# A conditioned two-layer block kernel in fp32: all LayerNorms and ssm products first, then the MLP by pairs of blocks

## The chip, the core and the metric

The kernel runs on one core of one Trainium2 chip. The metric is the device time of one execution in microseconds (us). The kernel before takes 586.52 us, the median of three runs (586.5 to 586.7). The engines are called as in the profile: PE is TensorE (PEld its weight loads), DVE VectorE, ACT ScalarE, POOL GpSimd and SP SyncE, which here only issues DMAs.

## What is computed

The input x has 2 batches of 2048 tokens of 512 values, and the condition has 512 values for each batch. All is fp32.

```python
emb = silu(cond) @ ada_w + ada_b
shift_msa, scale_msa, gate_msa, shift_mlp, scale_mlp, gate_mlp = split(emb, 6)
norm = ln(x) * (1 + scale_msa) + shift_msa
h = gelu(norm @ ssm_w1 + ssm_b1)               # 512 -> 512, exact gelu
x = x + gate_msa * (h @ ssm_w2 + ssm_b2)       # 512 -> 512
norm2 = ln(x) * (1 + scale_mlp) + shift_mlp
hf = gelu_tanh(norm2 @ ff_w1 + ff_b1)          # 512 -> 1024
x = x + gate_mlp * (hf @ ff_w2 + ff_b2)        # 1024 -> 512
```

Each of the two LayerNorms works over the 512 values of a token. Four matrix products follow: ssm1, ssm2, ff1 and ff2 below.

## The kernel before, in words

**Blocks.** The 4096 tokens are worked on in eight blocks of 512 (i = 0 to 7), four for each batch. A block's x is one SBUF tile of 128 x 4 x 512. The gates are folded into the weights w2 and fw2, which is done again for the second batch.

**A LayerNorm** (class Norm) has six steps: `stats` (DVE, bn_stats L511, one for each quarter c of the block; for block 1 they are shared with ACT, L525 to L534), `scales` (eight small operations on POOL, L580 to L598, that give rstd and -mean*rstd), `normal` (ACT, L612, four), `turn` (DVE, a transpose of 32 x 32 blocks, L623, four), `move` (L632, sixteen DMAs of 64 KB that carry the turned blocks to their partitions, issued by SP or by SP and ACT), `modulate` (ACT, L661, four, with shift and scale). What comes out has the features on the partitions.

**Products.** ssm1 and ssm2 use one Strassen level in Winograd's form: seven products P1 to P7 of four matmuls each, 128 x 256, in three PSUM banks (y, x, v) that are read and summed on as the products come (`group`, L474). The sums of operands that this needs are single tensor_tensor operations on DVE or POOL (L347). ff1 of block 0 is done in the same way, in two groups. From block 1 on, ff1 is `Second.products` (L1024): 26 products of two matmuls each, whose operands come from two lists of sums, HK_A for the weight (made once) and HK_B for the tokens (each block, L962). ff2 is `residual_in_leaves` from block 1 on: one Strassen level, of which P1 and P6 stay plain (L817, 16 matmuls of 256 columns) and the five others are split once more (L863, 70 matmuls of 128 columns).

**Order.** The order on every engine is written out by hand: each product group has hooks, lists of operations that are issued behind a named product. The blocks are interleaved: behind ff1 of block i comes ssm2 of block i+1, then ff2 of block i, then ssm1 of block i+2. So a block's normalisation, its sums and its DMAs lie beside other blocks' products. [...]

**Start.** Some idle matmuls (L1117) come first. Then the conditioning products (L274, "pada", sixteen small matmuls for each of six parts of ada_w), which need ada_w from DRAM. A gate product (L309, "pgate") copies the gate of batch 0 to all partitions.

**Lines that the prediction names:** L274 pada, L309 pgate, L395 folding of a gate into a weight, L474 ssm products, L817 plain and L863 split parts of ff2, L877 and L913 the readings of ff2's PSUM into x, L927 the last outputs, L1024 ff1.

Of the kernel before, what the change touches and what calls it, by code (L numbers as in the profile page):

```python
# [8 lines left out]
F32 = mybir.dt.float32  # L37
# [4 lines left out]

HK_A = [
    (1, '-', 1, 0),
    (3, '+', 3, 1),
    (11, 'n', 10, 11),
    (27, '+', 11, 1),
    (26, '-', 27, 8),  # L50
    (25, '+', 13, 15),
    (25, '-', 25, 12),
    (24, '-', 27, 2),
    (23, '-', 3, 24),
    (8, '+', 8, 23),
    (8, '+', 0, 8),
    (22, '-', 12, 26),
    (21, 'n', 1, 22),
    (22, '+', 2, 22),
    (9, '-', 9, 11),  # L60
    (20, '-', 6, 27),
    (10, '+', 6, 10),
    (19, '-', 9, 10),
    (19, 'n', 26, 19),
    (0, '-', 4, 0),
    (23, '-', 23, 0),
    (4, '+', 4, 27),
    (27, '-', 6, 19),
    (2, '-', 27, 2),
    (5, '+', 5, 11),  # L70
    (5, '-', 5, 4),
    (27, '+', 19, 25),
    (27, '-', 27, 5),
    (18, '+', 15, 1),
    (14, '+', 14, 15),
    (15, '-', 21, 14),
    (6, '-', 6, 11),
    (14, '-', 14, 27),
    (7, 'n', 7, 6),
    (6, '+', 7, 27),  # L80
    (6, 'n', 23, 6),
    (13, '-', 13, 5),
]
HK_B = [
    (23, '-', 4, 6),
    (22, '-', 0, 23),
    (21, '+', 1, 3),
    (20, '-', 21, 22),
    (19, '-', 7, 21),
    (18, '-', 5, 21),  # L90
    (17, '+', 3, 23),
    (16, '-', 18, 23),
    (15, '-', 19, 16),
    (14, '-', 17, 15),
    (13, '-', 20, 14),
    (0, '+', 0, 16),
    (12, '-', 6, 21),
    (11, '+', 2, 23),
    (1, '+', 1, 12),
    (10, '-', 11, 20),  # L100
    (9, '-', 12, 10),
    (8, '-', 16, 9),
    (2, '-', 2, 3),
    (7, '-', 6, 7),
]


HK_P = [
    (5, True, 26, 20, ((5, -1), (7, 1))),
    (3, True, 25, 3, ((5, 1), (7, 1))),  # L110
    (0, True, 12, 22, ((6, 1),)),
    (2, True, 1, 13, ((1, -1), (7, -1))),
    (5, False, 8, 21, ((1, 1),)),
    (0, False, 21, 0, ((7, 1),)),
    (1, True, 3, 19, ((1, 1),)),
    (2, False, 20, 15, ((3, -1),)),
    (0, False, 22, 18, ((1, 1),)),
    (3, False, 19, 17, ((5, -1),)),
    (2, False, 10, 14, ((5, 1),)),
    (5, False, 23, 12, ((3, 1),)),  # L120
    (0, False, 24, 16, ((0, 1),)),
    (1, True, 11, 8, ((0, -1), (2, -1))),
    (5, False, 4, 10, ((2, 1),)),
    (0, False, 2, 23, ((4, -1), (5, -1))),
    (3, False, 27, 1, ((3, 1),)),
    (5, False, 0, 9, ((0, 1),)),
    (1, False, 9, 11, ((4, 1),)),
    (4, True, 18, 14, ()),
    (3, False, 5, 2, ((2, 1),)),
    (0, False, 6, 6, ((2, 1),)),  # L130
    (4, False, 15, 5, ((7, -1),)),
    (3, False, 14, 4, ()),
    (0, False, 7, 7, ((3, 1),)),
    (3, False, 13, 11, ((6, 1),)),
]

HK_BANK = {5: "y", 2: "x", 4: "v", 0: "x", 1: "y", 3: "v"}
# [3 lines left out]
def kernel(  # L141
# [20 lines left out]
    KD = D // P  # L162
    KH = H // P
# [5 lines left out]
    NADA = ada_w.shape[1] // D  # L169

    const = ctx.enter_context(tc.tile_pool(name="const", bufs=1))
    big = ctx.enter_context(tc.tile_pool(name="big", bufs=7))
    sums = ctx.enter_context(tc.tile_pool(name="sums", bufs=3))
    work = ctx.enter_context(tc.tile_pool(name="work", bufs=1))
    small = ctx.enter_context(tc.tile_pool(name="small", bufs=3))
    dram = ctx.enter_context(tc.tile_pool(name="dram", bufs=1, space=bass.MemoryType.DRAM))
    ps_t = ctx.enter_context(tc.tile_pool(name="ps_t", bufs=2, space=bass.MemoryType.PSUM))
    ps_g = ctx.enter_context(tc.tile_pool(name="ps_g", bufs=2, space=bass.MemoryType.PSUM))

    ctx.enter_context(tc.manual_schedule())  # L180

# [4 lines left out]
    G = 32  # L186
    IDLE = 5


    R_COND, R_ADA = 0, B * KD  # L190
    R_B1 = R_ADA + NADA * KD
    R_FB1 = R_B1 + KD
    ROWS = R_FB1 + KH
    def big_tile(name):
        return big.tile([P, KD, D], F32, tag="big", name=name)

    xs = {}

    def load_x(i, pieces=1):
        xs[i] = big_tile(f"x_{i}")  # L200
        for s in range(pieces):
            c = slice(s * C // pieces, (s + 1) * C // pieces)
            nc.sync.dma_start(out=xs[i][:, c, :], in_=x_blk[i][:, c, :])

    ada = {}

    def load_ada(g):
        ada[g] = big_tile(f"ada_{g}")
        nc.sync.dma_start(
            out=ada[g], in_=ada_w[:, g * D : (g + 1) * D].rearrange("(k p) n -> p k n", p=P)  # L210
        )

    def load_w(name, w, t=None, eng=nc.sync):
        if t is None:
            t = const.tile([P, w.shape[0] // P, w.shape[1]], F32, tag=name, name=name)
        eng.dma_start(out=t, in_=w.rearrange("(k p) n -> p k n", p=P))
        return t

    def load_half(name, w, t, h):
        K = t.shape[1] // 2  # L220
        nc.sync.dma_start(
            out=t[:, h * K : (h + 1) * K],
            in_=w.rearrange("(h k p) n -> h p k n", h=2, p=P)[h],
        )

    def load_row(t, row):
        nc.sync.dma_start(out=t, in_=row.unsqueeze(0).to_broadcast([P, D]))
        return t


    fw2_t = const.tile([P, 5, 3, KD // 2, P], F32, tag="fw2_t", name="fw2_t")
    brows = fw2_t.rearrange("p a s k d -> p (a s k d)")[:, : KD * D].rearrange("p (k d) -> p k d", k=KD)
    rows = brows[:ROWS, 2, :P]
    nc.scalar.dma_start(out=rows[R_COND:R_ADA, :], in_=cond.rearrange("b (k p) -> (b k) p", p=P))
    nc.scalar.dma_start(out=rows[R_ADA:R_B1, :], in_=ada_b.rearrange("(k p) -> k p", p=P))
    nc.scalar.dma_start(out=rows[R_B1:R_FB1, :], in_=b1.rearrange("(k p) -> k p", p=P))
    nc.scalar.dma_start(out=rows[R_FB1:ROWS, :], in_=fb1.rearrange("(k p) -> k p", p=P))

    ident = const.tile([P, P], F32, tag="ident", name="ident")
    make_identity(nc, ident)  # L240
# [3 lines left out]
    w1_sb = load_w("w1", w1)  # L244
    load_x(1)
    load_ada(2)

    nc.gpsimd.memset(brows[:, :2, :P], 0.0)
    gate_b = {2: brows[:, 0, :P], 5: brows[:, 1, :P]}

    def load_gate_b(g):
        for m in range(P // G):
            row = ada_b[g * D : (g + 1) * D].rearrange("(n m q) -> m n q", n=KD, q=G)[m]
            nc.sync.dma_start(
                out=gate_b[g][m * G : m * G + B, :].rearrange("p (n q) -> p n q", n=KD),
                in_=row.unsqueeze(0).to_broadcast([B, KD, G]),
            )

    w2_sb = load_w("w2", w2)
    load_gate_b(2)  # L260
    b2_bc = work.tile([P, D], F32, tag="gb", name="gb2_0", bufs=2)
    load_row(b2_bc, b2)
    fw1_sb = load_w("fw1", fw1)
    load_ada(3)

    mods = {}

    def rows_of(g):

        pa = ps_g.tile([P, D], F32, tag="x", name=f"pada_{g}")  # L270
        w = ada[g].rearrange("p k (n m q) -> p k m n q", n=KD, q=G)
        for k in range(KD):
            for m in range(P // G):
                nc.tensor.matmul(  # L274
                    pa[m * G : (m + 1) * G, :P],
                    silu[:, k, :],
                    w[:, k, m],
                    start=(k == 0),
                    stop=(k == KD - 1),
                    tile_position=(0, m * G),  # L280
                    skip_group_check=True,
                )
        return pa

    def modulation(g0, part):

        g = g0 + part
        pa = rows_of(g)
        turned = pa[:, P : 2 * P]
        nc.vector.transpose(turned, pa[:, :P])  # L290
        turned = turned.rearrange("p (n q) -> p n q", n=KD)
        m = const.tile([P, KD, B], F32, tag=f"mod_{g0}_{part}", name=f"mod_{g0}_{part}")
        bias = colsT[:, R_ADA + g * KD : R_ADA + (g + 1) * KD]
        nc.vector.tensor_tensor(m, turned[:, :, :B], bias.unsqueeze(2).to_broadcast([P, KD, B]), ALU.add)
        mods[g0, part] = m

    gate, gate_rows = {}, {}

    def gate_rows_of(g, tag):
        pa = rows_of(g)  # L300
        r = work.tile([P, P] if g == 2 else [P, D], F32, tag=tag, name=f"grows_{g}", bufs=1)
        nc.vector.tensor_tensor(r[:, :P], pa[:, :P], gate_b[g], ALU.add)
        gate_rows[g] = r

    def first_ssm_gate():

        pg = ps_t.tile([P, D], F32, tag="t", name="pgate_2_0")
        for m in range(P // G):
            nc.tensor.matmul(  # L309
                pg.rearrange("p (n m q) -> p m n q", n=KD, q=G)[:, m],  # L310
# [62 lines left out]
    def thirds(t):  # L373
        return [t[:, j] for j in range(3)]
# [1165 lines left out]
```

## Time and profile before

| what | value |
|---|---|
| median of 3 runs | 586.52 us (586.5 to 586.7) |
| profiled execution, span from first to last instruction | 583.8 us |
| DMA traffic | 57.54 MB, mean 99 GB/s |
| DVE / ACT / POOL busy | 411.9 / 269.0 / 424.6 us |
| PE instructions recorded | 3287 |
| granted TensorE clock | 1.000 |

The profile is one execution. Its span leaves out what lies ahead of the first and behind the last instruction. A row of the timeline has start, length, engine, line, operation, output<-inputs, shapes and count, and in brackets the idle time ahead of it and who ended it. A row of the chain of work that ended last has start, length and what ran. A row of the groups has busy time and the mean of one in ns behind the count.

### The profile page before, as it was taken

The numbers are of one execution on the slowest core, as the hardware profiler recorded it, in microseconds if no ns is written. First come the engines' busy times: TensorE is split into PE (matmuls) and PEld (weight loads), VectorE is DVE, ScalarE is ACT, GpSimd is POOL, SyncE is SP. The second block draws the span as 40 slices with busy tenths as digits, with TensorE's granted clock in tenths as the row PEclk, the third lists the DMA queues.
The fourth block names the chain that finished last, engine by engine and source line by source line (L and its number), as shares of the span: only waits on it lengthen the run. The fifth ranks groups of instructions, "written<-read, shape, count | busy, mean of one in ns | idle before, by whom it ended". The sixth has DMA issues, their size and how long they took to land.

```text
span 583.8 us, 9508 instructions
## 1 busy us (share of the span) xinstructions
PE 577.3 (99%) x3287; PEld 514.4 (88%) x3287; DVE 411.9 (71%) x748; ACT 269.0 (46%) x495; POOL 424.6 (73%) x516
## 2 busy tenths in 40 slices
PE   9999999999999999999999999999999999999997
PEld 5788888888899888998889988898888998899896
DVE  4867898897867375685756857884756367787676
ACT  2644457405642554435742588235673331731520
POOL 1785249999997938969788799998579445369351
PEclk9999999999999999999999999999999999999999
DMA  8967332303205303472033821243130330031002
GB/s 322 394 186 290 92 72 74 108 37 108 61 15 180 127 0 69 118 213 73 1 90 74 288 73 24 50 122 122 45 72 2 100 118 1 1 72 74 1 1 72
DMA packets 26011, 57.54 MB, mean 99 GB/s; under 512 B 4928, under 2 KB 5996, under 8 KB 24300
## 3 DMA queue, kind: packets, MB, share of 16 engines
q1 hardware_dynamic: 22240, 52.20, 28.4%
q10 hardware_dynamic: 3724, 4.75, 3.3%
q8 instruction: 26, 0.43, 0.3%
q14 instruction: 21, 0.17, 0.1%
HBM read 32.80 MB, written 8.40 MB: 71 GB/s over the span
## 4 chain that ended last, share of the span: by engine, by line
PE 94%; DMA 3%; DVE 2%; issue 0%; ACTq 0%; DVEq 0%
PE px_hC L1024 10%; PE py_oA L474 9%; PE py_hA L474 9%; PE py_hC L1024 8%; PE py_oC L817 8%; PE pv_hC L1024 8%; PE pl_oC_P_y L863 8%; PE pv_oA L474 5%; PE pl_oC_P_v L863 5%; PE pv_hA L474 4%; PE pl_oC_P_x L863 3%; DMA ada<-in_L_cond_ada_w_dram 3%; PE px_oA L474 2%; PE py_oC L474 2%; PE py_hC L474 2%; PE px_hA L474 2%
## 5 line engine op out<-in xcount | busy, mean ns | idle before, releaser
L661 ACT ACTIVATE nT<-nT,mod,mod 128x512 f32<-128x512 f32 x36 | 26.4, 803 | 63.4 <-DMA nT<-blocks 57.2
L347 POOL TENSOR_TENSOR hSC<-hClo,hChi 128x512 f32<-128x512 f32 (+1 forms) x16 | 19.7, 1234 | 41.0 <-ACT hChi L1019 35.6
L962 POOL TENSOR_TENSOR forms<-forms 128x256 f32<-128x256 f32 x56 | 41.8, 746 | 3.3
L511 DVE BATCH_NORM_STATS2 st<-x 128x6 f32<-128x512 f32 x56 | 37.9, 677 | 5.1 <-DMA x<-in_x_dram 4.9
L1024 PE MATMUL py_hC<-forms,fw 128*128 128x256 f32 x168 | 41.0, 380 | 0.0
L1041 DVE TENSOR_TENSOR hClo<-hClo,py_hC 128x512 f32<-128x512 f32 x42 | 28.6, 684 | 15.3 <-ACT hClo L1038 9.4
L1024 PEld LDWEIGHTS py_hC<-forms,fw 128*128 128x128 f32 x168 | 31.7, 190 | 4.7 <-DVE hClo L1041 0.2
L623 DVE STREAM_TRANSPOSE blocks<-nT 128x512 f32<-128x512 f32 x36 | 24.9, 703 | 13.5 <-ACT nT L612 13.5
L612 ACT ACTIVATE nT<-x,nmr,rstd 128x512 f32<-128x512 f32 x36 | 27.0, 805 | 13.5 <-POOL nmr L598 13.5
L661 ACT ACTIVATE x<-x,mod,mod 128x512 f32<-128x512 f32 x24 | 17.6, 802 | 32.8 <-DMA x<-blocks 32.8
L580 POOL TENSOR_SCALAR ve<-mv 128x4 f32<-128x4 f32 x16 | 3.7, 234 | 39.2 <-DVE mv L512 36.8
L962 POOL TENSOR_TENSOR forms<-nT,forms 128x256 f32<-128x256 f32 x42 | 30.5, 746 | 0.5
L962 POOL TENSOR_TENSOR forms<-nT 128x256 f32<-128x256 f32 x14 | 10.4, 740 | 28.2 <-ACT nT L661 23.8
L1041 DVE TENSOR_TENSOR hChi<-hChi,pv_hC 128x512 f32<-128x512 f32 x35 | 23.3, 681 | 10.4 <-PE pv_hC L1024 6.7
L1024 PE MATMUL px_hC<-forms,fw 128*128 128x256 f32 x112 | 27.6, 379 | 0.0
L1019 ACT ACTIVATE hClo<-hClo,colsT 128x256 f32<-128x256 f32 x56 | 25.3, 498 | 5.0 <-DVE hClo L1041 4.8
L877 DVE TENSOR_TENSOR x<-pl_oC_P_y,x 128x256 f32<-128x256 f32 (+1 forms) x66 | 24.7, 375 | 2.9 <-PE pl_oC_P_y L863 1.2
L474 PE MATMUL py_oA<-w,hA 128*128 128x256 f32 x112 | 26.5, 379 | 0.0
L1038 ACT ACTIVATE hChi<-py_hC 128x512 f32<-128x512 f32 x14 | 7.6, 594 | 40.9 <-PE py_hC L1024 40.8
L778 DVE TENSOR_TENSOR x<-pv_oA,x 128x512 f32<-128x512 f32 x16 | 11.0, 688 | 21.6 <-PE pv_oA L474 10.5
L1019 ACT ACTIVATE hChi<-hChi,colsT 128x256 f32<-128x256 f32 x56 | 25.1, 496 | 1.9 <-DVE hChi L1041 1.9
L1038 ACT ACTIVATE hClo<-px_hC 128x512 f32<-128x512 f32 x21 | 12.5, 596 | 28.1 <-PE px_hC L1024 23.2
(345 smaller groups left out, 1813.2 us busy)
## 6 DMA issues: line engine op xcount, KB each, us to landing
x<-in_x_dram SPq DMA_DIRECT2D x13, 1024.0 KB
out_dram<-x SPq DMA_DIRECT2D x14, 512.0 KB
ada<-in_L_cond_ada_w_dram SPq DMA_DIRECT2D x6, 1024.0 KB
x<-blocks SPq DMA_DIRECT2D x96, 64.0 KB
nT<-blocks SPq DMA_DIRECT2D x88, 64.0 KB
fw<-in_L_cond_ff_w_dram SPq DMA_DIRECT2D x2, 2048.0 KB
nT<-blocks ACTq DMA_DIRECT2D x56, 64.0 KB
w<-in_L_cond_ssm_w_dram SPq DMA_DIRECT2D x3, 1024.0 KB
```

The costliest lines, as they stand in the source:

```text
L474: nc.tensor.matmul(ps[b][j * apart][:, j, :], lhs(p, j, k), rhs(p, j, k), start=(fresh and j * (not apart) == 0 and k == 0), stop=(p in (" ...
L511: nc.vector.bn_stats(st, xs[self.i][:, c, :])
L612: nc.scalar.activation(t, x_c, AF.Identity, bias=self.nmr[:, c : c + 1], scale=self.rstd[:, c : c + 1])
L623: nc.vector.transpose(self.bl[:, :, :, c, :].rearrange("p m k q -> p k m q"), self.nT[:, c, :].rearrange("p (k m q) -> p k m q", k=KD, m=C),)
L661: nc.scalar.activation(dst, src, AF.Identity, bias=shift, scale=scale)
L817: yield lambda j=j, k=k: nc.tensor.matmul(ps[BANK[p]][:, j, :], hops(p, j, k), wops[p][:, k, :], start=False, stop=(k == kdim - 1), skip_g ...
L863: nc.tensor.matmul(t[:, n, :], hops.leaves[p][f][:, k, :], leaf_wops[p][f][:, k, :], start=room not in started, stop=(f in ("P2", "P3", "P ...
L877: nc.vector.tensor_tensor(d, src, d, ALU.add)
L962: eng.tensor_tensor(reg[d], reg[a], reg[b], ALU.add if f == "+" else ALU.subtract)
L1019: nc.scalar.activation(h, h, AF.Gelu_apprx_tanh, bias=fb1T[:, m : m + 1])
L1024: nc.tensor.matmul(ps[b][:, j, :], fa[ra][:, j * P : (j + 1) * P], fb[rb].rearrange("p a (c q) -> p c a q", q=Q), start=(fresh and j == 0) ...
L1041: nc.vector.tensor_tensor(dest(d), dest(d), ps[b], op)
```

## The change

The body of the kernel is written anew. What it computes for a block stays the same but for ff1; the diff below has the core of it.

1. **Order of stages.** First all eight blocks go through LayerNorm 1, ssm1, ssm2 and LayerNorm 2 (up to its turned blocks). Then four pairs of blocks go through ff1 and ff2.
2. **ff1 by pairs.** A pair is 1024 tokens. The product is taken by two nested Strassen levels: seven outer products (OUTER), each by seven inner ones (CARRIED), so 49 leaves of two matmuls of 256 columns. Two outer products are interleaved, leaf by leaf. The outer sums on the token side are outer_s, the inner ones inner_s; those of the weight are made once (`weight_fw1`), by DVE or POOL.
3. **Through DRAM.** The seven parts of the weight (128 x 7 x 256 each) are written to DRAM by weight_fw1. For each pair they are read back, through three slots of 7 kB for each partition (`ring`). Block results of ssm (x1_d) and the turned blocks of LayerNorm 2 (turned_d) go through DRAM too: ff2 reads its x1 again, `normed2` reads the turned blocks and modulates them.
4. **SBUF by hand.** Regions named turned, ring, hidden, near, far, rows and fw2 are shared between uses; a later use waits for the earlier one. For one, block 1's and block 6's x stand in the ring region at 14 to 22 kB, where parts of the weight (0 to 21) and the inner sums (21 to 27) come later.
5. **A planner orders the instructions.** Every operation is recorded with its reads and writes, its engine or engines, a cost and a latency (class `Plan`). Due times are set backwards from the order of the matmuls, which stays as written, and a list schedule then chooses for each engine what is next. Sums of two SBUF operands ("vg") may be put on DVE or POOL. The result is a fixed order for each engine and for the SP and ACT DMA queues.
6. **Smaller parts.** All of block 1's statistics are on DVE. The conditioning product of gate_msa comes behind all of ssm1(0). The two last outputs are both issued by SP. ff2 of block 0 is in leaves as well, and both blocks of a pair use the same form.

```diff
-HK_A = [
...
-HK_P = [
...
+class Plan:
...
+    def order(self):
...
+        return sorted(ops, key=lambda op: (op.start, op.n))
...
+    turned_r, ring_r, hidden_r = region("turned", 28), region("ring", 27), region("hidden", 32)
+    near_r, far_r, rows_r = region("near", 27), region("far", 27), region("rows", 16)
+    fw2_r = region("fw2", 43)
...
+    x1_d = [far(f"x1_{i}", P, C, D) for i in range(NBLK)]
+    turned_d = {i: far(f"turned_{i}", P, C, D) for i in SOON}
+    fw1_d = far("fw1_parts", 7, P, 7, W)
...
+    slots = [kb(far_r, 16, 8), kb(ring_r, 14, 8), kb(rows_r, 0, 8), kb(rows_r, 8, 8), kb(fw2_r, 34, 8)]
+    xs = [cut(slots[i % 5], "p (c d) -> p c d", c=C) for i in range(NBLK)]
...
+    FW1_AT = {"P1": 0, "P7": 1, "P2": 2, "P4": 3, "P5": 4, "P6": 5, "P3": 6}
+    OUTER = ("P1", "P2", "P6", "P7", "P4", "P3", "P5")
+    def weight_fw1():
...
+        outer = first(outer_quarters(t), thirds(s), cuts=2)
+        for n, p in enumerate(OUTER):
...
+            first(q, thirds(s_in))
+            first_four = cut(w, "p c (r h) -> p c r h", r=2)
+            dma(fw1_d[n, :, :4].rearrange("p (c r) h -> p c r h", c=2), first_four)
+            dma(fw1_d[n, :, 4:], s_in)
...
+    inner_s = [cut(kb(ring_r, 21 + 3 * n, 3), "p (s a r) -> p s a r", s=3, a=C) for n in range(2)]
+    ring = [cut(kb(ring_r, 7 * n, 7), "p (f h) -> p f h", f=7) for n in range(3)]
...
+        def prepare(n):
+            w = ops[OUTER[n]]
...
+            inner[n] = second(q, thirds(inner_s[n % 2]))
+            slot[n] = ring[(7 * s + n) % 3]
+            dma(slot[n], fw1_d[n])
...
+            for h in range(2):
+                mm(t[:, h, :], slot[n][:, FW1_AT[f], h * P : (h + 1) * P], src, f in ("P1", "P5") and h == 0, f in ("P2", "P3", "P4"))
...
+            elif p == "P5":
+                d = cut(both(quad), "p (o t) c -> p o t c", o=2)
+                tt("v", d, t.unsqueeze(1).to_broadcast([P, 2, 2, HT]), d, ALU.add)
...
+        for at in range(7 * 6 + 2 * 6 + 1):
+            for n in range(7):
+                if at == 7 * n:
+                    prepare(n)
+                if at >= 7 * n and (at - 7 * n) % 2 == 0 and (at - 7 * n) // 2 < 7:
+                    leaf(n, (at - 7 * n) // 2)
...
+    hid = {0: ssm1(0, tok[0], w1_ops)}
+    plan.anchor = plan.ops[anchor]
+    gate_rows_of(2, 1)
+    w2_ops = weight2(0, 2)
...
+    ssm2(0, hid[0], w2_ops, PLAIN)
+    norm2(0)
...
+    hid[1] = ssm1(1, tok[1], w1_ops)
+    tok[3] = norm1(3)
+    gate_rows_of(5, 1)
+    hid[2] = ssm1(2, tok[2], w1_ops)
+    weight_fw1()
     for i in range(1, NBLK):
...
+        ssm2(i, hid[i], w2_ops)
+        if i in SOON:
+            norm2(i)
+        if i == 4:
+            ff = weight_fw2(0, 1)
+        if i + 1 == PER_B:
+            w2_ops = weight2(1, 1)
+        if i + 2 < NBLK:
+            hid[i + 2] = ssm1(i + 2, tok[i + 2], w1_ops)
+    for s in range(NBLK // 2):
+        if 2 * s == PER_B:
+            ff = weight_fw2(1, None)
+        ff1(s)
...
+        for blk in range(2):
+            ff2(s, blk, *ff)
+
+    for op in plan.order():
+        op.fn(plan.engines[op.on])
```

`first` and `second` are the four sums of one Strassen level (Winograd's form) for the one and the other operand. `both` gives a quarter of the second block's hidden values in both halves, so that one reading of P5's PSUM adds to 1024 columns. The names of the lines in the changed kernel differ; the prediction names stages instead: ssm1(i), ssm2(i), norm2(i), ff1 of a pair, ff2(i).

More of the change, by code (lines that the diff above doesn't have):

```diff
@@ L243 @@
     load_ada(1)
-    w1_sb = load_w("w1", w1)
-    load_x(1)
+    load_w(w1_t, w1)
     load_ada(2)
[L248 to L256, printed above, removed]
-            )
@@ L259 @@
[L259 to L310, printed above, removed]
-                picks[:, m, :],
-                gate_rows[2],
-                start=True,
-                stop=True,
-            )
-        gate[2, 0] = pg
@@ L1125 @@
[L1125 to L1136 removed]
+    memset(half_t, -0.5)
+    memset(silu, 0.0)
+    act(marks[0][:, 52:56], half_t, AF.Silu)
+    for g in (2, 5):
+        memset(gate_b[g], 0.0)
+    memset(leaf_row, 0.0)
@@ L1137 @@
+    act(
+        cut(silu[:, :, :B], "p k b -> p b k"),
+        cut(cols_t[:, R_COND:R_ADA], "p (b k) -> p b k", b=B),
         AF.Silu,
```

1931 lines of the change are left out of this document (818 added, 1113 removed).

## Prediction

> **What bounds the kernel now.** I read the page first, then the list of TensorE's waits, then the chain of work that ended last. The page says that TensorE is busy in 99% of the span, at nine tenths or more in all slices but the last, and that 94% of the chain is TensorE. The span is 583.8 us; the median time is 586.52, so 2.7 us lie around the span, and all sums below are spans plus these 2.7.
>
> ```profile
> span 583.8 us, 9508 instructions
> PE 577.3 (99%) x3287; PEld 514.4 (88%) x3287; DVE 411.9 (71%) x748; ACT 269.0 (46%) x495; POOL 424.6 (73%) x516
> PE   9999999999999999999999999999999999999997
> PEclk9999999999999999999999999999999999999999
> PE 94%; DMA 3%; DVE 2%; issue 0%; ACTq 0%; DVEq 0%
> ```
>
> The list of TensorE's waits has two entries, 2.3 us in all (columns: total, times, longest):
>
> ```profile
> PE idle L1117 <- POOL ident masks.py:199: 1.3, 1, 1.3
> PE pada L274 <- DMA ada<-in_L_cond_ada_w_dram: 1.0, 1, 1.0
> ```
>
> So every product is ready before TensorE wants it. The time is the number of matmuls times their spacing, and a change is worth what it takes off that number, less any wait that it opens. The spacing stands in the chain (start, length, what). Five rows are the starts of one block's period: second MLP product, first ssm product of the next block but one, first MLP product, second ssm product, and the next period.
>
> ```profile
> 165.34 3.45 PE py_oC L817 x16
> ...
> 174.48 2.23 PE pl_oC_P_x L863 x20
> ...
> 187.88 1.73 PE py_hA L474 x8
> ...
> 199.97 0.86 PE py_hC L1024 x4
> ...
> 222.42 1.73 PE py_oA L474 x8
> ...
> 234.50 3.45 PE py_oC L817 x16
> ```
>
> Each matmul instruction leaves two records. An ssm product takes 199.97 - 187.88 = 12.09 us (28 matmuls of 256 columns, 0.4317 each), the 26-product MLP stage 222.42 - 199.97 = 22.45 (52 matmuls, 0.4317 again), the leaf form of the second MLP product 187.88 - 165.34 = 22.54 (16 of 256 columns, 70 of 128; ten leaves take 2.23).
>
> **The change, part by part.** *Matmuls.* Before: 16 ssm products x 12.09 = 193.4; seven first MLP products x 22.45 = 157.2; seven second ones x 22.54 = 157.8; block 0's two of 56 matmuls, 48.4. Together 556.8. After: 193.4 again; four pairs of blocks, 49 leaves of two matmuls of 256 columns each, 4 x 98 x 0.4317 = 169.3; eight second products, 180.3. Together 543.0. **The products save 13.8 us.**
>
> *What stays around them.* The rows of TensorE's timeline (start, length, engine, line, what):
>
> ```profile
> 1.34 6.68 PE L1117 MATMUL idle<-ident 128*128 128x512 f32 x8 [1.34 <-POOL ident masks.py:199]
> 7.96 0.26 PE L1126 MATMUL rowsT<-ident,fw_t 44*128 44x44 f32 x1
> ...
> 14.76 1.94 PE L474 MATMUL py_hA<-nT,w 128*128 128x256 f32 x8
> ...
> 21.13 1.08 PE L274 MATMUL pada<-ada,silu 128*32 128x128 f32 x32 [0.98 <-DMA ada<-in_L_cond_ada_w_dram]
> ...
> 23.98 1.05 PE L309 MATMUL pgate<-grows,fw_t 128*128 128x128 f32 x8
> 25.01 1.97 PE L474 MATMUL py_hA<-nT,w 128*128 128x256 f32 x8
> ...
> 42.45 1.08 PE L274 MATMUL pada<-ada,silu 128*32 128x128 f32 x32
> 43.46 1.99 PE L474 MATMUL py_hA<-nT,w 128*128 128x256 f32 x8
> ```
>
> ```profile
> 579.02 0.61 PE L863 MATMUL pv_oC<-fw_t,hSC 128*128 128x128 f32 x4
> ```
>
> The first product starts at 14.76, and its predecessors stay as they are. Four conditioning products (1.0 each) and one gate product (1.0) are 5.0. As a test, before: 14.8 + 556.8 + 5.0 + the 1.0 of the wait = 577.6, against the last matmul's end, 579.02 + 0.61 = 579.6. I carry the missing 2.0 over. After, without new waits: 14.8 + 543.0 + 5.0 + 2.0 = 564.8.
>
> *Wait 1, start of ssm product 2 of block 0: 1.0.* The changed order puts the gate's conditioning product behind all of block 0's first product (ends 26.9) instead of in its midst. Its sum on DVE, the gate product and another conditioning product follow; half of this chain lies beside TensorE's own work. Bounds 0 and 2; I take 1.0, so ssm2(0) runs from 31.5.
>
> *Wait 2, ssm1(1): 7.8.* This is the largest that the order shows. In the kernel before, block 1's LayerNorm has its statistics by 23, split between DVE and ACT. Its rows on POOL, ACT, DVE and the two queues give the length of each step:
>
> ```profile
> 23.23 0.37 POOL L580 TENSOR_SCALAR ve<-mv 128x4 f32<-128x4 f32 x1 [1.84 <-ACT unread L534]
> ...
> 26.19 0.23 POOL L598 TENSOR_SCALAR nmr<-nmr 128x4 f32<-128x4 f32 x1
> ```
>
> ```profile
> 26.45 2.93 ACT L612 ACTIVATE nT<-x,nmr,rstd 128x512 f32<-128x512 f32 x4 [2.59 <-POOL nmr L598]
> ...
> 32.84 5.10 ACTq L632 DMA_DIRECT2D nT<-blocks  x8
> 40.75 2.93 ACT L661 ACTIVATE nT<-nT,mod,mod 128x512 f32<-128x512 f32 x4 [8.11 <-DMA nT<-blocks]
> ```
>
> ```profile
> 32.06 0.70 DVE L623 STREAM_TRANSPOSE blocks<-nT 128x512 f32<-128x512 f32 x1
> ```
>
> In the changed order all four statistics are on DVE. Two come only behind the sum that waits for the conditioning product (26.9 + 1.0 + 0.4 = 28.3). The other two stand behind the reading of ssm2(0)'s first product, which is not done before 31.5 + 1.7 = 33.2. With 0.7 for that reading and for each statistic they end at 36.4. From there: scales 26.42 - 23.23 = 3.2, so 39.7 (with a semaphore's 0.1); normals 2.9, 42.7; last transpose 0.7, 43.4; sixteen 64 KB moves from first issue to modulation, 40.75 - 32.84 = 7.9, so 51.4; the two modulations that the first matmul needs, 1.0 more: 52.4. TensorE has finished ssm2(0) at 43.6 and one conditioning product at 44.6. Bounds: 5 (half the statistics earlier by an idle stretch) and 9. While it waits, everything queued on TensorE behind it waits too; nothing else is ready there.
>
> *Waits 3 and 4, ssm1(2) and ssm1(7): 1.6 each (0 to 3).* Block 2's normals are behind evictions on ACT, and eight of its moves are issued by ACT in line; the same chain ends 1.6 behind TensorE. Block 7's sixteen moves are all issued by SP. There the row of SP's queue prices it: 10.0 for sixteen against 5.1 for eight on each of two queues.
>
> ```profile
> 423.35 10.01 SPq L632 DMA_DIRECT2D x<-blocks  x16
> ```
>
> *Wait 5, from ssm to the MLP: 6.* The inner sums of the first pair share SBUF with block 6's x, so the first of them must come behind the last transpose of norm2(6). On DVE this is ordered behind the last reading of ssm2(7), a gate product, four statistics of norm2(7) and three weight sums. I price that with these rows (busy, mean ns), DVE's first; the two of POOL serve further down:
>
> ```profile
> L511 DVE BATCH_NORM_STATS2 st<-x 128x6 f32<-128x512 f32 x56 | 37.9, 677 | 5.1 <-DMA x<-in_x_dram 4.9
> L962 DVE TENSOR_TENSOR fw<-fw 128x256 f32<-128x256 f32 x11 | 8.7, 793 | 0.1
> L877 DVE TENSOR_TENSOR x<-pl_oC_P_y,x 128x256 f32<-128x256 f32 x44 | 18.5, 420 | 1.6 <-DVE x L828 0.5
> L913 DVE TENSOR_TENSOR x<-py_oC,x 128x1024 f32<-128x1024 f32 x7 | 8.6, 1224 | 0.2
> ```
>
> ```profile
> L962 POOL TENSOR_TENSOR forms<-forms 128x256 f32<-128x256 f32 x56 | 41.8, 746 | 3.3
> L347 POOL TENSOR_TENSOR hSA<-hA 128x512 f32<-128x512 f32 x6 | 7.7, 1277 | 0.0
> ```
>
> A sum of 256 columns lies between 0.42 (reading PSUM) and 0.79 (beside a busy POOL); I take 0.42, as POOL has little to do there. Last reading 0.85 behind the last ssm matmul, gate 0.7, four statistics with their aggregations 3.1, three weight sums 1.3, transpose 0.7, two inner sums 0.8: 7.4, while the second leaf is wanted at 0.86. One weight sum may lie ahead of it all, so I take 6. Bounds 2 (the statistics run ahead in DVE's idle time) and 9 (the sums at 0.79, and ACT's normals of norm2(6), which stand behind the copy of the first leaf, late too).
>
> *Wait 6, the parts of the first MLP weight: 8 (0 to 12).* Each pair reloads seven parts of 0.92 MB from DRAM into three slots; SP issues them in order. In the first pair, part 2's slot is under block 6's x, and parts 4 and 6 stand behind norm2's stores, which wait for DVE as above. The steady demand is small: 6.4 MB in 42.3 us is 152 GB/s, and the window of the start shows 339 (last two columns: DMA share, GB/s).
>
> ```profile
> 0.00:20.00 20.00, 18.66 (x123) 12.23 (x123) 11.95 (x30) 7.15 (x14) 7.97 (x16) 1.00 0.92 339
> ```
>
> So only the first pair's order costs: 0.5, some 4.5 and 2.5 to 3. The later pairs load behind free slots, at nothing.
>
> *Steady MLP.* A pair takes 42.3 + 45.1 = 87.4 on TensorE. Its 36 sums of 256 columns at 0.746 and 40 of 512 at 1.277 come to 78 if POOL did all, and DVE is free to take part. No wait, except at the end of each first product, where the readings of 1024 columns (1.22 by the row above) come every 0.86: 4 x 0.5 = 2.0 (0 to 5). Refolding the second weight before pair 2: 1.0 (0 to 3).
>
> *Start after a long wait: 3.0.* In the row at 1.34 above, the first four matmuls of 512 columns take 6.6 us up to the next instruction at 7.96, against 4 x 0.863 at the spacing of later ones: 3.2 lost while TensorE starts from idle. The wait of 1.0 at 21.13 was followed by no such loss. I book 3.0 for one restart, behind wait 2, and nothing for the shorter ones; bounds 0 and 9 (three waits over 4 us). [...]
>
> *End.* The last reading, the output and the rest are 583.8 - 579.6 = 4.2 now; both last outputs go to SP instead of SP and ACT, one issue of 0.4 more.
>
> ```profile
> 580.20 0.38 SPq L927 DMA_DIRECT2D out_dram<-x  x1
> 580.20 0.46 ACTq L927 DMA_DIRECT2D out_dram<-x  x1
> ```
>
> **Sum.** 564.8 + 1.0 + 7.8 + 1.6 + 1.6 + 6 + 8 + 2 + 1 = 593.8; restart 3.0, end 4.6: span 601.4; plus 2.7: **604.1 us**, 17.6 slower than now, since 32 us of waits and restart stand against 13.8.
>
> **The rivals.** *A, the MLP part runs without a wait (584).* Place: the four pairs. If norm2(7)'s work on DVE is early enough that the first inner sums and loads are there, waits 5 and 6, the ends (2.0) and the refold (1.0) are gone, 17; with no restart seen either, 3: 604.1 - 20 = 584. For it: DVE is busy 71% of the span, DMA demand is half of what the start moved. Against: the order on DVE and SP is fixed, and the shared SBUF forces it. It decides if these terms together stay under 2.4 instead of 20.
> *B, only the hand-over is hidden (590).* The waits 5 and 6 shrink, because 12 us of earlier waits let DVE and SP catch up: 604.1 - 14 = 590.
> *C, more restarts (614).* Two more restarts (6) and wait 6 at its upper end (4).
> *The saving does not come:* if a leaf of the new product took longer than 0.863, each 0.1 would cost 196 x 0.1 = 20 us; the same operand shapes ran at 0.4317 in 52 of 52 above, so I give it no chance of its own; it is part of C.
>
> **How the numbers follow.** The forecast's case (597 to 611) has 0.53, B (588 to 597) 0.19, C (above 611) 0.12, A (below 585.3) 0.13, and 0.03 fall within 0.2% of now, which is about what a measurement of this kernel can tell from no change. Slower: 0.53 + 0.19 + 0.12 = 0.84. For 8 in 10 the range goes from A's 584 to 612: it leaves out half of A and most of C.
>
> **What would show it.** In the profile of the changed kernel: TensorE's busy time lower by some 14 us; a list of TensorE's waits with ssm1(1) (behind the modulation or the moves' DMA) near 8 us at about 45 us of the span; a hole at the hand-over near 235 us, released by DVE's inner sum and by loads of the weight parts; slices below 9 at both places and none in the last three pairs; the matmuls behind the first hole at half rate for some us. It would be wrong if block 1's statistics run before the gate's sum, or if the first pair shows no wait on the ring's loads.

## The result, and the profile after

The changed kernel takes **665.9 us** (663.4 to 666.6, four runs) against 586.5 (586.2 to 586.7): 13.5% more, a ratio of 1.135 with a 95% interval of 1.133 to 1.137. The forecast was 604.1 with a range of 584 to 612. The direction was right, and the loss is four and a half times what was forecast. The profiled execution took 666.6 with a span of 664.8.

The page of the changed kernel, the lines that answer to those shown of before:

```profile
span 664.8 us, 9308 instructions
PE 586.9 (88%) x3291; PEld 514.4 (77%) x3291; DVE 486.8 (73%) x865; ACT 240.5 (36%) x414; POOL 349.8 (53%) x415
PE   8979996998997773681789999999999999999997
PEclk9998997999999688885989999999999999999999
PE 53%; DMA 15%; DVE 12%; SPq 11%; POOL 4%; issue 2%; ACT 1%; ACTq 0%; DVEq 0%
```

Three things are to be seen. The gaps lie in the first half, and from slice 22 on PE is at nine tenths or more in all slices but the last. The granted clock, 9 everywhere before, falls to 5 to 8 beside the gaps. And half of the chain of work that ended last is no longer PE: DMA, DVE and SP's queue have 38%.

TensorE's waits in the changed kernel (total, times, longest):

```profile
PE bank L280 <- DMA ring<-fw_parts: 27.2, 3, 16.4
PE bank L280 <- DVE hidden L242: 18.9, 10, 7.0
PE bank L280 <- DVE ring L242: 14.0, 2, 10.4
PE bank L280 <- ACT turned L260: 6.3, 3, 4.2
PE bank L280 <- DVE far L242: 1.8, 1, 1.8
```

The whole list adds up to 73.1 us, against 2.3 before. With the order of the matmuls, which is fixed, each wait can be put to its product:

| wait ahead of | forecast | measured | released by |
|---|---|---|---|
| gate product and ssm2(0) | 1.0 | 0.8 | DVE, ACT |
| last product of ssm2(0) | 0 | 1.75 | DVE |
| ssm1(1) | 7.8 | 4.25 (starts at 51.1, forecast 52.4) | modulation on ACT |
| ssm1(2), ssm1(7) | 1.6 each | 0.7, 1.4 | modulation on ACT |
| last products of ssm1(3), ssm1(5), ssm1(7), ssm2(6) | 0 | 5.8, 2.5, 7.0, 3.6 | DVE |
| second leaf of ff1, first pair (hand-over) | 6 | 10.4 | DVE, inner sum |
| weight parts, first pair | 8 | 5.8, 16.4, 5.0 | DMA |
| ends of the four ff1 | 2.0 | 0.55 to 0.96 each | DVE, POOL |
| refold of the second weight (the wait lies in ff2(4), at its reading of PSUM) | 1.0 | 1.1 | DVE |

The account of the span, 664.8 - 583.8 = +81.0: the matmuls -13.8; waits 73.1 - 2.3 = +70.8; half clock +17.9 (the record of the granted clock has pieces of 3.41 us and multiples of it at 0.5, in which PE was busy for 35.8 us, so half of that is lost, as in the four matmuls below that take 3.78 us and not 1.89); the other 6.1 are not waits, as PE's idle stretches of any length add up to 73.5, but nearly all busy time. An estimate for a part of it: the row of an uncut ssm product is 12.25 us long and the next one starts after 12.09, so a wait behind a product shows some 0.16 of its end; with 24 waits more than before that is 3.8. The rest was not looked for.

One sign in the prediction did not show because of this: TensorE's busy time did not fall by 14 us but rose by 9.6, from 577.3 to 586.9, as the half clock (17.9) and these busy times hide the 13.8 that the matmuls saved.

**One of the unforeseen waits, step by step.** The chain of the changed kernel from 90 to 112 us (start, length, what):

```profile
90.67 0.54 SPq L301
91.26 12.18 DMA turned<-far
103.46 2.49 DVE far L523 x4
105.95 1.22 DVE marks L483 x2
...
107.96 0.60 DVE hidden L242
108.61 3.78 PE bank L280 x8
```

The same place on the timeline of DVE and of PE:

```profile
103.46 2.49 DVE L523 STREAM_TRANSPOSE far<-turned 128x512 f32<-128x512 f32 x4 [7.54 <-DMA turned<-far]
```

```profile
91.93 10.90 PE L280 MATMUL bank<-turned,ring 128*128 128x256 f32 x48
108.61 3.78 PE L280 MATMUL bank<-turned,ring 128*128 128x256 f32 x8 [5.78 <-DVE hidden L242]
112.18 12.89 PE L280 MATMUL bank<-near,hidden 128*128 128x256 f32 x56
```

Read upwards: the last four matmuls of ssm1(3) wait for a reading of PSUM on DVE ("hidden"). DVE had been idle for 7.5 us, but in its order four transposes of the next block stand ahead of that reading, and they wait for a buffer. The buffer is one of the two that all turned blocks go through. A norm2 before them has it until its store to DRAM has landed, 12.2 us after the issue. Then the four matmuls take 3.78 us, twice what they take elsewhere (1.89): the half clock.

How fast these stores run, in a stretch where they are alone (columns as before; the last two are DMA share and GB/s):

```profile
100.00:103.00 3.00, 2.83 (x14) 2.14 (x12) 0.00 (x0) 0.32 (x1) 0.00 (x0) 1.00 0.27 103
```

A share of 0.27 is 4.3 of 16 DMA engines; the packets in the trace say nearly the same, 3.9 of 2 KB under way on average in this stretch. The store's DMAs are written with an outer index of 4 (`"q a r -> a q r"`).

The waits for the weight parts have the same origin. SP's queue in the changed kernel, first pair of ff1:

```profile
271.69 5.01 SPq L301 DMA_DIRECT2D ring<-fw_parts  x2
279.50 1.00 SPq L301 DMA_DIRECT2D fw_parts<-fw  x2
281.67 11.80 SPq L301 DMA_DIRECT2D turned<-far  x6
293.51 2.47 SPq L301 DMA_DIRECT2D rows<-x  x1
296.03 3.05 SPq L301 DMA_DIRECT2D turned<-far  x2
299.19 4.78 SPq L301 DMA_DIRECT2D ring<-fw_parts  x2
```

The load that PE wants at 297 is issued at 299 behind eight of norm2's stores, and lands at 313.9, behind them in the queue too: in the trace 199 of the 256 packets of the two loads issued there are through by 309.5, and the others come mostly two to four at a time, as the stores did, which end at 311.4.

### The profile page after: what moved, and what is told of

The parts are those of the page before. It is cut to its first block, busy times and chain, and to the rows that moved or that the text cites. A ratio compares the mean times of both kernels' runs of the same rounds, so it can differ in the third digit from the quotient of the medians.

```text
span 664.8 us, 9308 instructions
## 1 busy us (share of the span) xinstructions
PE 586.9 (88%) x3291; PEld 514.4 (77%) x3291; DVE 486.8 (73%) x865; ACT 240.5 (36%) x414; POOL 349.8 (53%) x415
## 3 DMA queue, kind: packets, MB, share of 16 engines
q10 hardware_dynamic: 844, 1.07, 0.7%
## 4 chain that ended last, share of the span: by engine, by line
PE 53%; DMA 15%; DVE 12%; SPq 11%; POOL 4%; issue 2%; ACT 1%; ACTq 0%; DVEq 0%
PE bank L280 53%; SPq L301 11%; DMA turned<-far 11%; DVE hidden L242 4%; DVE far L523 3%; DMA ring<-fw_parts 2%; POOL near L242 2%; DVE rows L242 1%; DVE fw L242 1%; ACT turned L260 1%; DVE marks L483 1%; DMA fw<-in_L_cond_ff_w_dram 1%; DVE near L242 1%; DMA fw<-in_L_cond_ff_b_dram 1%; DVE ring L242 0%
## 5 line engine op out<-in xcount | busy, mean ns | idle before, releaser
L280 PE MATMUL bank<-turned,ring 128*128 128x256 f32 x896 | 219.6, 396 | 49.6 <-DMA ring<-fw_parts 27.2
L280 PEld LDWEIGHTS bank<-turned,ring 128*128 128x128 f32 x896 | 175.2, 198 | 82.4 <-DMA ring<-fw_parts 28.4
L242 DVE TENSOR_TENSOR hidden<-bank,hidden 128x512 f32<-128x512 f32 (+1 forms) x170 | 125.7, 757 | 57.1 <-PE bank L280 54.4
L242 DVE TENSOR_TENSOR rows<-bank,rows 128x256 f32<-128x256 f32 (+3 forms) x234 | 99.1, 458 | 28.3 <-PE bank L280 22.6
L280 PE MATMUL bank<-near,hidden 128*128 128x256 f32 x448 | 101.9, 389 | 5.8 <-DVE ring L242 3.6
L280 PEld LDWEIGHTS bank<-near,hidden 128*128 128x128 f32 x448 | 87.4, 196 | 19.7 <-DVE ring L242 4.0
L280 PE MATMUL bank<-ring 128*128 128x256 f32 x336 | 86.0, 393 | 13.7 <-DVE ring L242 10.4
L280 PE MATMUL bank<-fw,hidden 128*128 128x128 f32 (+1 forms) x512 | 80.1, 301 | 0.0
L280 PEld LDWEIGHTS bank<-fw,hidden 128*128 128x128 f32 x512 | 72.9, 191 | 3.9
L280 PE MATMUL bank<-fw,far 128*128 128x128 f32 (+2 forms) x624 | 66.6, 286 | 1.1 <-POOL marks L490 1.0
L242 POOL TENSOR_TENSOR hidden<-hidden 128x512 f32<-128x512 f32 (+1 forms) x34 | 47.5, 1399 | 34.5 <-ACT hidden L260 24.2
```

The costliest lines, as they stand in the source:

```text
L242: lambda E: E.tensor_tensor(o, a, b, f),
L280: lambda E: E.matmul(o, lhsT, rhs, start=start, stop=stop, skip_group_check=True, **kw),
```

## The experiments

All but two ran once, beside a run of the kernel before, on several chips, where that kernel took 585.6 to 586.6 us. The changed kernel's own runs spread over 3.2 us, so only differences well above that are read from times alone. "In the changed kernel's own order" means that every engine's order is that of the changed kernel.

**e1_even_store.** The store of norm2 in one DMA over 128 partitions. The planner sees four stores as before, so the order stays; the first of them issues the whole block and the others nothing. The block is then read back by four DMAs instead of one:

```diff
-    turned_d = {i: far(f"turned_{i}", P, C, D) for i in SOON}
+    turned_d = {i: far(f"turned_{i}", C, P, D) for i in SOON}
...
-            dma(turned_d[i][m * G : (m + 1) * G].rearrange("q a r -> a q r"), bl[:, m, :])
+            dma(turned_d[i][m], bl[:, m, :])
+            plan.ops[-1].fn = lambda E, m=m: m or E.dma_start(out=turned_d[i].rearrange("m p r -> p m r"), in_=bl)
...
             dma(t, turned_d[i])
+            plan.ops[-1].fn = lambda E: [
+                E.dma_start(out=t[m * G : (m + 1) * G], in_=turned_d[i][m].rearrange("(a q) r -> q a r", q=G))
+                for m in range(C)
+            ]
```

> The changed kernel in its own order of instructions, with one thing other: norm2's turned blocks of a block go to DRAM by one DMA of 1 MB whose outer index is the 128 partitions, instead of four of 256 KB whose outer index has 4 steps; the permutation is made when they are read back (four DMAs of 32 partitions). Theory S (the store): in the changed kernel these four move about 105 GB/s together and land 12 to 15 us behind their issue; until then one of the two turning buffers is held, DVE waits in line for it, and the PSUM readings behind it on DVE are late. So here the waits ahead of the last products of ssm1(3), ssm1(5), ssm1(7) and ssm2(6), 18.9 us together, go, the hand-over (10.4) shrinks to about 5 and the ring's 27.2 to about 10, and with them about two thirds of the half-clock time: 605 to 625 us. Rival Q (SP's queue of issues, 0.63 us each, is the limit): 3 of some 26 issues of a block less, 650 to 660. Rival B (the sheer traffic, 108 MB against 57.5): no change, 666.

Measured: **620.1 us, 46 less**, as theory S said. Its waits (total, times, longest):

```profile
PE bank L280 <- DVE hidden L242: 11.4, 8, 5.3
PE bank L280 <- DVE ring L242: 6.6, 1, 6.6
PE bank L280 <- ACT turned L260: 6.2, 3, 4.3
PE bank L280 <- DMA ring<-fw_parts: 4.2, 2, 4.1
```

No wait is left ahead of the last products in the ssm part, the hand-over is 6.6 (6 in the prediction) and the loads of weight parts cost 4.2. The store in this kernel, DMA share and GB/s in the last columns:

```profile
91.00:94.00 3.00, 2.88 (x12) 1.91 (x11) 2.65 (x6) 2.41 (x5) 0.00 (x0) 1.00 0.98 314
```

A load of x, issued at 90.65, 0.65 us behind the store, shares this window; in the changed kernel, where it was issued at 92.53 behind the stores, 92 to 96 us show a share of 0.39 and 107 GB/s. The store has the same bytes, and the rate in the window is three times as high. In the packets sixteen are under way (0.98 of 16 is 15.7) where there were four. PE was busy in half clock for 18.0 us instead of 35.8. Rivals Q and B are out.

**e8_even_four.** As e1, read back in the same way, but with four stores of 256 KB each:

```diff
-            dma(turned_d[i][m * G : (m + 1) * G].rearrange("q a r -> a q r"), bl[:, m, :])
+            dma(turned_d[i][m], bl[:, m, :])
```

> As e1_even_store, in the changed kernel's own order, but still four DMAs of 256 KB for a block's turned values, each with the 128 partitions as its outer index. It parts the spread of a store over DMA engines from the number of issues. If the spread is what counted, the time is that of e1_even_store within 5 us: 616 to 626. If it was the three issues less on SP, it is nearer to the changed kernel: 645 to 668.

Measured: 619.8 us. The number of issues is without weight: 0.3 us lie between e1 and e8. What e1's and e8's stores share, and the changed kernel's don't, is the outer index of 128 and with it the spread over DMA engines, a DMA share of 0.98 and of 1.07 against 0.27 (an x load, issued at 91.78, is in e8's window too):

```profile
91.00:94.00 3.00, 2.83 (x12) 1.85 (x12) 2.61 (x6) 2.63 (x4) 0.00 (x0) 1.00 1.07 356
```

**e2_told.** The planner's size of these stores times three (it reckons with 330 GB/s, where the trace shows 103):

```diff
+    def dma(o, a, q="s", slow=1):
+        size = slow * max(cols(o.unsqueeze(0)), 1) * 4
...
+            dma(turned_d[i][m * G : (m + 1) * G].rearrange("q a r -> a q r"), bl[:, m, :], slow=3)
```

> The changed kernel with the same instructions, but the planner is told that norm2's stores are three times as long, so that it orders around them. Theory S: the stores still hold the buffers, but work that doesn't need them comes first; a part of the waits goes, 625 to 655 us. If the order alone was at fault (rival O), nearly all waits go: about 600. Rival Q and B: within 10 us of 666.

Measured: 649.2 us. With about the true length in the plan the waits for "hidden" go from 18.9 to 3.8, but those for weight parts stay (31.0). So a good third of the loss to the stores (17 of 46) goes with an order made for stores of their real length; the rest stays as long as the stores are slow.

**e3_both_queues.** Half of norm1's moves go to ACT's queue:

```diff
+                if m % 2:
+                    moves.append(plan.ops[-1])
...
-        op.fn(plan.engines[op.on])
+        op.fn(plan.engines["a" if op in moves else op.on])
```

> The changed kernel in its own order, but half of the sixteen moves of every norm1 (those of odd m) are issued by ACT. Rival Q: a block's moves take 5 us of issuing instead of 10, so the ssm part's waits shrink by half or more: 630 to 645 us. Theory S: the stores are as slow as before and hold the buffers: 655 to 668, the ssm1(1) and ssm1(2) starts unchanged as they are issued so already.

Measured: 667.9 us. So SP's issues, though its queue stands in the chain with 11% of the span, did not set the time. They were not without effect: the waits for "hidden" halved, from 18.9 to 9.0, but those for the modulation rose from 6.3 to 12.7 and those for "rows" from 1.1 to 6.5.

**e4_fill.** Idle matmuls in the waits. What this filling, and that of e7 and e12 below, writes goes in part to PSUM banks that hold live values, so what these three kernels compute is wrong and only their times are used:

```diff
+            count, bank = fills.get((op.note, n), (0, 0))
+            for _ in range(count):
+                nc.tensor.matmul(
+                    cut(banks[bank], "p (c q) -> p c q", c=C),
+                    ident,
+                    ident.unsqueeze(1).to_broadcast([P, C, P]),
+                    start=True,
+                    stop=True,
+                )
```

> The changed kernel in its own order, with 60 matmuls of 512 columns (0.85 us each) whose result nobody reads, put on PE ahead of the matmuls that wait over 3.4 us: 4, 6, 7 and 3 in the ssm part (ssm1(1), ssm1(3), ssm1(7), ssm2(6)) and 11, 6, 18 and 5 in ff1 of the first pair. Theory C (after an idle stretch PE runs at half rate for pieces of 3.4 us, which cost some 23 to 26 us here): the half clock is gone from the record, the real products take their 0.4317 again, and the time falls to 640 to 650 us although PE has more to do. Rival N (the half clock is hidden in the waits, as DVE and the DMAs set the pace anyway): 660 to 670.

Measured: 671.2 us, above the ranges of both theories. PE was busy in half clock for 20.1 us instead of 35.8, worth 7.9, but the 51 us of filling overran the waits that were left, and one filling itself waited 5.4 us for a bank. It settles nothing on the time.

**e7_fill_even.** The same with 20 matmuls in e1's four longest waits.

> e1_even_store with 20 matmuls of 512 columns that nobody reads, ahead of the four longest waits: 4 ahead of ssm1(1), 7, 4 and 5 in ff1 of the first pair. They are 17 us of work within waits of 20. Theory C (half clock after idle): the half-clock windows go, of which 18 us held matmuls, so the time falls by up to 9, to 611 to 615. Rival N (the pace is set by DVE and DMA there, the half clock costs nothing): 619 to 625.

Measured: 615.8 us, 4.2 less than e1; in half clock PE was busy for 3.4 us instead of 18.0. Half of the 14.6 is 7.3; the 3 that are missing may be filling that overran its wait. That is 0.8 above theory C's range and 3.2 below the rival's, and only a little more than the spread of single runs.

**e6_slots** and **e5_slots_even.** The x of blocks 6 and 7 elsewhere, without and with the even store:

```diff
-    xs = [cut(slots[i % 5], "p (c d) -> p c d", c=C) for i in range(NBLK)]
+    xs = [cut(slots[i], "p (c d) -> p c d", c=C) for i in (0, 1, 2, 3, 4, 0, 2, 3)]
```

> The slots of e5_slots_even alone, with the changed kernel's own slow stores. If the hand-over (10.4) and part of the ring's waits come from the shared SBUF: 640 to 655, the ssm part as before. If they come from the stores alone: 660 to 670.

> e1_even_store's store, ordered by the planner itself, and block 6's and block 7's x in the slots of blocks 2 and 3 instead of 1 and 2, so that the inner sums and the weight ring of the first pair share no SBUF with block 6's x. My theory of the hand-over (shared SBUF puts the first inner sum behind norm2(6)'s last transpose): the hand-over wait of 6.6 us goes to under 2, the ring's waits shrink, less half clock: 600 to 612. Rival (the hand-over waits for DVE's work as such): 614 to 622.

Measured: 655.6 us, just above the first range given for it, and 623.3. In both the wait of the second leaf is gone. Waits of e5_slots_even:

```profile
PE bank L280 <- DVE rows L242: 12.1, 5, 6.4
PE bank L280 <- ACT turned L260: 10.4, 4, 5.1
...
PE bank L280 <- DMA ring<-fw_parts: 1.0, 1, 1.0
```

No "DVE ring" stands there any more, and the loads wait for 1.0. So the shared SBUF made the hand-over's wait, as the prediction had it. But the new slots come free later: ssm1(6) now waits 5.1, ssm1(7) 2.9 and ff2(0) 6.4, and e5's time lies above the ranges of both theories.

**e9_slots2** and **e10_x1.** Both have the even store of 1 MB, known to the planner, and the slots in the order 0, 1, 2, 3, 4, 1, 0, 2; in e10 block 1's x is also loaded as the fifth MB:

```diff
+    xs = [cut(slots[i], "p (c d) -> p c d", c=C) for i in (0, 1, 2, 3, 4, 1, 0, 2)]
...
+                if op.note == "norm1 1" and op.size > self.BULK:
+                    op.late = 10000.0
```

> The even store of 1 MB ordered by the planner, and the slots of x dealt out so that block 5 follows block 1 in the ring region and block 6 follows block 0: the ring region is free one block earlier, and no x is loaded later than its chain allows. If the shared SBUF makes the hand-over and the first pair's ring waits, and e5_slots_even's new waits (ssm1(6) 5.1, ssm1(7) 2.9, ff2(0) 6.4) came from x's later slots, both kinds go: 594 to 608 us. If the later waits come back in another place whatever the slots (rival: DVE's and SP's work there is too much): 615 to 625.

> e9_slots2 with block 1's x loaded as the fifth MB instead of behind ada_w's later parts, w2 and the bias row, so that all its statistics lie on DVE ahead of the sum that waits for the gate's conditioning product. My step 'wait 2' says that the wait at ssm1(1) comes from there: with it the wait (4.3), most of the 1.7 ahead of ssm2(0)'s last product and the half clock behind them (1.7) go: 6 to 8 us below e9_slots2. Rival (the chain of moves and modulation is too long anyhow): within 3 us of it.

Measured: 614.4 (6 over the expected range's end: the start of ssm1(5) waits 1.6, and 3.6 show up in ff2(4), where the refold's wait was) and **605.8**, 8.6 below it, where 6 to 8 were expected. In e10's trace all four statistics are through by 23.5, ahead of the gate's sum at 28.5, and the waits at ssm2(0)'s end and at ssm1(1) are gone; so they did come from block 1's statistics behind that sum. 3.1 of them come back at ssm1(2).

**e11_x1_both_queues.** e10 with half of all norm1's moves planned on ACT's queue.

> e10_x1 with the moves of every norm1 shared between SP and ACT, which the planner knows. With the stores even, the waits left at the starts of ssm1(5) and ssm1(7) (1.5 and 1.9, and half clock behind the second) lie behind sixteen moves in line on SP. If SP's issuing is what is late there: 600 to 603 us. If ACT's own work is delayed as much by eight issues (rival): 604 to 609.

Measured: 613.3 us, slower than both theories said. ssm1(7) waits 4.0 instead of 1.9, and ff2(4) 6.9. The planner's order changed together with the queue, so this run doesn't tell the two theories apart.

**e12_x1_fill**, then **e13_x1_again** and **e14_x1_fill_again**, the last two timed in rounds.

> e10_x1 in its own order with ten matmuls that nobody reads: four of 512 columns ahead of ssm1(2) (wait 3.1), two ahead of ssm1(7) (1.9) and four of 384 columns in ff2(0) (2.8), the three places behind which the record shows half clock, 15.6 us of matmuls in it together. Theory C: half of these 15.6, 7.8 us, are lost to the clock; the filling takes 7.7 us of which all but some 1.5 lie in waits: 598 to 601. Rival N (the clock's loss is made up elsewhere): 604 to 608.

> e10_x1 once more, timed in rounds on the same chip as e14_x1_fill_again: 603 to 608 us, and half-clock windows behind the same waits.

> e12_x1_fill, with the filling in ff2(0) put so that it accumulates in unused columns. Theory C: 3 to 7 us below e13_x1_again, outside both kernels' spread, with next to no half-clock window left. Rival N: within 2 us of it.

Measured: e12 601.6; e13, the same kernel as e10, 603.3 (601.4 to 603.9); e14 601.5 (601.1 to 604.8). By time alone e13 and e14 can't be told apart: the medians differ by 1.9 us, which is what rival N said (within 2), and theory C's 3 to 7 us were not borne out. The traces say why. The 28 matmuls of ssm1(2), in e10, in e13 and in e14:

```profile
62.04 15.37 PE L282 MATMUL bank<-turned,ring 128*128 128x256 f32 x56 [3.09 <-DMA gates<-hidden]
```

```profile
62.06 14.31 PE L282 MATMUL bank<-turned,ring 128*128 128x256 f32 x56 [3.11 <-ACT turned L262]
```

```profile
58.90 3.70 PE L1110 MATMUL bank<-far 128*128 128x512 f32 x8
62.44 12.26 PE L282 MATMUL bank<-turned,ring 128*128 128x256 f32 x56
```

After the same wait the same kernel lost 3.1 us in one execution and 2.0 in the other (on another chip); with four idle matmuls in the wait it lost none. Over the whole run PE was busy in half clock for 15.6 us in e10's profile, for 3.4 in e13's (601.4 us in that execution) and not at all in e14's. So the half clock is real, and filling can take it away, but it does not always: the mean granted clocks of e14's other three executions are 0.994 to 0.997, where 1.000 means none and one piece of 3.41 us makes 0.997; e13's four are 0.990 to 0.997. And e14 has 7.7 us of filling to pay.

What differs when the same wait brings a piece in one execution and none in another can be read from the granted clock that the traces record. In the changed kernel's the eight stretches of half clock within the span, 19 pieces, start on a grid of 3.413 us, to within 1 ns; so do those of the experiments' 13 traces that have any. What goes with them is how long PE idles within one step of this grid. In the changed kernel it is 2.40 us or more in the step ahead of each of the eight stretches, and at most 1.75 in every step that full clock followed. In all 14 traces, in the step ahead of the 63 stretches of half clock, it is never under 1.76 us, and every step of full clock with more than 2.01 us was followed by one; between the two it went either way. The wait of 2.84 us in ff2(0) had 2.10 of it in one step in e10 (half clock) and was cut into 1.94 and 0.90 in e13 (none). This was found in the traces afterwards; no run moved a wait against the grid to test it.

e14 has the lowest median. It is still 2.7% slower than the kernel before (ratio 1.0275, 1.0246 to 1.0305), with 16.9 us of waits, none over 1.6 us.

## Why the prediction was wrong

1. **What bounds the kernel, and the saving:** right. The steady pairs run as worked out. ff1 of the second pair starts at 391.62 and takes 43.65 us, against 42.3 by the forecast and 0.96 for the wait at its end, as the timeline of PE in the changed kernel has it:

```profile
434.34 1.10 PE L280 MATMUL bank<-ring 128*128 128x256 f32 x4 [0.96 <-DVE hidden L242]
435.27 4.06 PE L280 MATMUL bank<-fw,hidden 128*128 128x256 f32 x20
```

   The ends and the refold, forecast at 3.0, cost 3.0 + 1.1.
2. **Waits 1 to 4:** the mechanism was right (e10 takes wait 2 away), the sizes too large: 12.0 forecast, 7.2 measured, and 1.75 more ahead of ssm2(0)'s last product. Wait 2's chain came out nearly as worked out: scales from 36.4 and normals from 39.5, forecast 36.4 and 39.7, then 7.05 for the moves instead of 7.9, so that ssm1(1) starts at 51.1 instead of 52.4. The wait is shorter mostly because TensorE itself comes later, at 46.9 instead of 44.6. That the start of the scales agrees is in part luck: the terms named for the statistics, 33.2 and three times 0.7, give 35.3, not 36.4; the aggregations left out there, a reading that starts at 33.9 and a sum that held POOL until 36.3 made up for it.
3. **Wait 5, the hand-over:** place and mechanism right (e5, e6: it goes with the shared SBUF). 6 forecast, 10.4 measured, 6.6 with even stores: by e1 the part above 6 was the stores.
4. **Wait 6 is the step that failed.** I priced the loads from the start's 339 GB/s and said that parts 4 and 6 "stand behind norm2's stores, which wait for DVE". That they stand behind them was right. What I left out was the stores' own time: I gave the four stores of norm2 no price at all, though the change adds them to each block's path. They move 103 GB/s and land 12 us later. The waits came to 27.2 against 8, and to 4.2 in e1. The slow stores did it together with the shared SBUF: with the same stores and other slots (e6) 11.4 are left.
5. **A wait that isn't in the prediction:** the last products in the ssm part, 18.9 us. It is the same omission seen from SBUF: two buffers for sixteen turned blocks, one held by each store. I had asked of each moved step what SP issues for it, but not how long the DMA holds what it reads. e1 and e8 show it: with every compute engine's order as it was, only the form of the stores and of their reading back changed, and 46 us went.
6. **The restart:** half right. I booked 3.0 for one restart from a row of the start, bounds 0 and 9; it was 17.9, as eight waits, of 3.6 to 16.4 us, each brought half clock, 3.4 to 17.1 us of it. That is 2.2 for each: what was mis-sized is the number of restarts, more than the price of one. The length of a wait alone does not tell whether half clock follows: it did behind one of 1.9 (e10, ssm1(7)), and did not behind one of 3.6 (e9, in ff2(4)). The first lay within one step of the grid described above, the second was cut into 1.90 and 1.71.
7. **The rivals:** A, B and C all lay too low. Their common base was the sum with too few waits; none of them had a store.

With even stores (e1) the sum can be tried again: 604.1 forecast, 620.1 measured, which is still 8 above the range's end, so the stores were not the only term mis-sized. Its list of waits holds 36.8, of which 2.3 were there before, so 34.5 against 29.0; its half clock is 9.0 against 3.0. The other 4 or 5 us are of the size of the unexplained busy time above. What is open: where that time lies, what sets the position of the grid, and whether the some 15 us of waits that e14 has beyond those of the kernel before can be scheduled away.

## What to carry to other kernels

A DMA's price is not its bytes over the best rate in the profile: look in a trace at how many DMA engines its form keeps busy (here an outermost index of 4 kept four, at 103 GB/s, one of 128 sixteen, at 314 GB/s with an x load beside it), and count the time for which it holds its source. Where a kernel is full on one engine, a new wait is paid for in two ways, by itself and by the slower clock behind it (here 70.8 and 17.9 us); so a saving of 2% in instructions is only worth having if no wait of some us comes with it. An order that a planner makes is as good as its worst duration: one store priced three times too fast put readings of PSUM behind a buffer that was not free.

## What was not expected of the hardware

- Four 256 KB stores with an outer index of 4 ran at 103 GB/s with a DMA share of 0.27; with 128 partitions as the outer index a window with the same bytes and an x load in it showed 314 GB/s (e1) and 356 GB/s (e8), with a share of 0.98 and 1.07.
- The clock falls to 0.5 for multiples of 3.41 us, and one wait can bring several: beside the 16.4 us wait of the first pair, 17.1 us in one stretch, most of it inside the wait. Waits of 1.9 and 2.84 us brought a piece in one execution and none in another of the same kernel (e10, e13); of the second, 2.10 lay in one step of the grid of 3.413 us in e10, and 1.94 and 0.90 in two steps in e13.
